# Expert sizes for every set, unscaled token rows, centred weights in DRAM and a folded skip term in a two-layer mixture-of-experts kernel

## The chip, the cores and the metric

The kernel runs on one core of a Trainium2 chip. The metric is the time of one execution on the device in microseconds. A core has a matrix engine (TensorE, in the profile PE, with its weight loads as PEld), a vector engine (VectorE, DVE), a scalar engine (ScalarE, ACT), a general engine (GpSimd, POOL) and a queue engine (SyncE, SP) that issues transfers here. Each takes its own instructions strictly in order; what one engine makes for another is announced with semaphores.

## The reference

The input x is 16 sequences of 256 tokens with 128 features, 4096 tokens in all. Four steps follow one another, with residual additions.

```python
# 1 attention: the softmax over m sums to one and v does not depend on m
att = softmax(q k^T * scale, axis=2)
opt = einsum('blmh,blhd->blhd', att, v)          # = v
x = x + opt_of(layernorm(x)) @ w_out.T + b_out

# 2 and 4: a mixture of experts, the same weights both times
n = layernorm(x)
logits = n @ gate_w                              # 8 experts
top2, weights = top-2 of logits, softmax over the two
x = x + sum_i weights_i * relu(n @ w1[e_i]) @ w2[e_i]   # 128 -> 512 -> 128

# 3 a selective-scan mixer (W_x, W_dt, A_log, D, W_out, b_out)
y = scan(u, delta, A, B, C) + u * D              # the skip term
x = x + y @ W_out.T + b_out
```

The above is cut to what matters: attention reduces to a linear map of the normalised tokens; each token goes to the two of eight experts with the highest logits, and what the experts return is weighted by a softmax over the two; the mixer's last term is the input u scaled by D for each feature.

## The kernel before

**Blocks and sets.** The 4096 tokens are 8 blocks of 512 (four tiles of 128 tokens each). A mixture-of-experts layer does not run over all blocks at once. It runs over sets of blocks: in layer 1 the sets are [0], [1], [2,3], [4,5], [6,7] (`FIRST`, L28), in layer 2 [0,1], [2,3], [4,5], [6], [7] (`SECOND`, L29). `layer` (L1679) does for each set: what comes before (attention, or the gate of layer 2), `route`, `experts`, and then what comes behind: `arrive` (L1659, return of the experts' rows and the mixer) in layer 1, `finish` (L1667, return, transposes and output) in layer 2.

**Routing.** `choose` (L1156) finds the two highest logits of each token as one-hot rows and the softmax factors p. A few bf16 multiplications count, for every token, how many tokens ahead of it in the set chose the same expert. From this comes a slot for each of the token's two experts. `route` (L1330) then makes a normalised and scaled row of the token for each of the two, (x − mean) · rstd · p, on ACT or DVE (tile `row`), and an indirect transfer on POOL (`scatter`, L876, seen as L880) writes 128 such rows at a time to their slots in a DRAM buffer `slots`. As relu passes a positive factor, scaling a row by p is the same as weighting what the expert returns.

**Experts.** Every expert has a fixed number of slots in a set, given by `SLOTS` (L32) as rows and columns, (108, 3) being 324 slots; the program's matrix shapes follow from it, and not from the counts of the run. `experts` (L1389) fetches an expert's slots to the tile `xs` (SP), transposes them (into `ps_b`, copied to `xsT`), multiplies by the four 128-wide parts of w1 (the up multiplications, into `ps_B` or `ps_b`), applies relu on ACT or DVE (`h`), multiplies by the four parts of w2 (the down multiplications, into `ps_y`), transposes back (`yT`, `ps_b`, `yr`) and stores the rows to a DRAM buffer `ys` (SP). For some sizes the down multiplication is turned round and gives rows at once (`ps_y<-w_s,h`). The weights of all eight experts stay in on-chip memory (`w1_s`, `w2_s`). Set [0] of layer 1 is dealt with otherwise: `dealt` (L1316) makes a one-hot matrix of slots and tokens for each expert (`u<-ramp`) and multiplies, with no transfer.

**Return.** `collect` (L1446) fetches, for each block and each of the two choices (a half), four times 128 rows of `ys` by indirect transfers on POOL (`gather`, L889, seen as L892) into the tile `yy`, and adds the 128x512 tile to x on DVE or POOL.

**Ranked sizes.** In layer 2 the sizes in a set differ from expert to expert. `ranking` (L1253) sorts the experts by their counts in the first set of layer 2 and the order holds for all its sets (`RANKED`, L44). `load_experts` (L921) therefore loads the weights a second time in that order, 16 transfers of 256 KB, whose source address is read from a register (a `value_load` on SP for each expert). In layer 1 all experts have the same size in a set.

**Order.** All work is first recorded as jobs of a `Plan` (L239) and then emitted in an order that is packed in the string `ORDER` (L62): a rank for each job. The plan's own durations (`cost`, and those given with `scatter`, `gather`, `move`) decide which engine takes a job that several could do, and how long TensorE is expected to idle ahead of a job. Where that is over 0.5 us, multiplications of zeros are sent in their place, one for 0.26 us (L1705, here called fillers); within the first 5 us (`COLD`) half as many. A memset of one element (L1711) stands between neighbouring indirect transfers of one kind. As all instructions are issued by one helper, nearly all lines of the profile are L772, and tiles tell the groups apart.

**Fallback.** If a count exceeds its slots, or a bound that the mixer's shortened scans rest on fails, a second program (`general`, L433) computes everything again (L1718 to L1730).

Of the kernel before, what the change touches and what calls it, by code (L numbers as in the profile page):

```python
# [11 lines left out]
BF16 = mybir.dt.bfloat16  # L12
# [7 lines left out]
P = 128  # L20
# [12 lines left out]
    {  # L33
        "first": ((88, 2),) * 8,
        1: ((84, 2),) * 8,
        2: ((108, 3),) * 8,
    },
    {
        "first": ((126, 3), (112, 3), (108, 3), (98, 3), (96, 3), (88, 3), (126, 2), (117, 2)),
        1: ((98, 2), (91, 2), (88, 2), (80, 2), (84, 2), (75, 2), (70, 2), (128, 1)),  # L40
        2: ((126, 3), (117, 3), (110, 3), (104, 3), (108, 3), (96, 3), (90, 3), (126, 2)),
    },
)
RANKED = (2,)  # L44
UNIT = 2
JOIN = 2

COLD = 5.0
# [14 lines left out]
    "c-qZZ2V4_p|G(!F2uWCBZ^GVNMD}nMWhmmpRjsY4t)oufI_lQiswi$nt>RvFf>K)%!~%*UB1=HoJFEa1cmE`Jxw{}(`+wi}^LZ0U"  # L63
    "a?kVJZ+?H@-|v>G_^I*=>c6NNCEAl^pxer^W>rkfI9&R;>iv%8rd7`B9lu02joA1NUDGqgsne+5m*>sC|3s_)i)v%K>WE364%f`z"
    "G%9VWd>|BeK0IC08FfuyS$#TV!ssUsJvZ9pw@tBaV2TlOKM(^Ype&9CWvPXsXYyKG+Pu%zXlZI1Sm&A}IY4CALbDer*&iR4gwV&l"
    "%_}jzc_s5zX!X3PvIWf#4x)X!&c}M*s#~aW*_FM4<>R>>-Ss7LRsE&oXUE3!i@n2)%YK;$2Ux%Q=KJd&AzO97EXmqll<=(G$|n86"
    "dYcDRExkEyN=&Uj^@^>Aca=O|2u`0WZ*KkZPp*nx>bjin<VsZC<o=9uRhFUFl+z=MPhNm~zw4pXzFM^_s$-IHUykn8ElEaxc^26-"
    "@4I$-U9_@v4^`W~w0Z1KeP?YmwJLUVr{|Jk*2t*vvi=>escnr%S2%5T@YvyUd1cK_&1T~j6D^|8^}R6ZVc4@5r`2UVu#9lkK^d>j"
    "<5raWMYj1fEzYZOy26KDMUnzv7Ki#3$Js3MGeWdkH_RQX!$+g^SGwX*L0g)m*&ht^hr`B{m+-Z+MtiQ=%kQlyO?ID9`_|x>g>x4a"
    "7{0aWT9KvwE7Mny<Gx<_BC^rwXq|G-%~+*L?XOC-N_X*TlWs>d*t>6dr4MgmZ>V5Cdl#UwvuaJIa7A;6SkO9NyAy2)R#I*_c4irG"  # L70
    "f$}i1aA)c7s#VilXwygk=1!Yh4K5@zA4WBp!hdS2*QXZDe|&PBD<YV-*P?Y!iDl#0qE3S>ix*QK?M<<E=x(XAp(VMh1?XG@R;LUe"
    "^+r5mvX*|O{~BSeh+)#r_1}t5_Zhr&a6Vyi`WybF4oh}yO!N4+5htCOsU-6w+usb|b1Ki@BBPCK;{T?1ty+gYBRIVexWd-=;yaSJ"
    "&s)c$pQk1Mu(kK>{gXydj2^f9i*!A>vkJ$Aory7?vCXs9d*QbqY<=vPD_5viZHRw+xyi_Maei$clW%G}<<Bhkhz`r&MH-;Cg^e&a"
    "U3gYoEtvixd0S^(bWqX_ezZ?DQW4gCxKZW)U-sXiwFV<^9XWugj&I$OH!^<jINSI_Rp(0X8CAy1J2}<+XY8MsQOzx+FI`ck!)UF1"
    "r{3=xWR>+`>d7lshLx35&odZn7Zx}mrDnxJanplDErz>)?7F~R3+C+aA5-pJSJA{omZhmanOZhgkCAfdi0_(u)pB)q^G@34(G14f"
    "eS4#Xe51_BB9U#NK~YP9t>|iZM^tyo*>WS%F&D1MxJN(sPW#RtZCBBJZJ^)!epUT0n_AeiD}P#^{fyO-2NJ+a(?751T|Dt?cbC&s"
    "Vc(n$QTC>HM#at;b;t51I;SD3MmT%!f%h}4>PBvxuFe>3;@b3@A8^VmYfe%~m6J|SeG|jhc2S6Tkp)nnb$DNx$-9k@&62&})9eDh"
    "ScjD#Mm+6S`}*KmrOj)ty&MV-D)rOH_rKCv)^PRbMmOGYj!yTV8??Q`+N`UlY#O%f5B};74O>|C*7x@ozso+too$4EyDPAtJ-2Le"
    "uTEEI%<mI*o7jdlVWH_fj=;E{yK8^RlKf4p9e+HX@qI@>qK&dre+c0=@TMCTa6xyst-wJ;H>2N&$y}<c%!q`U@CUzomIp^G>DPJt"
    "S!x=E$jI-zmAMAtYp?dBF3J<a_^i}!9^FgHm{tEc#Gh9&w{A|0ef5VbPi>8y1=e34J|A%@QR|nJJQv~V+30jzx^DxA@33*RbCs>%"  # L80
    "ef3A`HOopwyjkjeHH}(F$Ieng4b!X;HExa5f1%a}jGt%hF>5F+ZFknJV%x@_61{ioY8P?EddV{*+HUb(fS#Qbt)^2r^(WJ`)UPYu"
    ")JFWl;98WeIb=8Tk2<=R1-&Pa79=`8w;g#um40nvvTte-sCm{D_|vkM$>|}6bRG!cYgMZ0^S*OreBm=TH+%Z~Jcp5~?Y_@P(9st@"
    "2CsX<E{?mh@~%t6aDJ(4L*w;>xy$qNjg9mfd=Ae^*L+-(bAJ8d=)3ycVdKZQ%egm9ODFqhX5N_LFyCI_K3f0nvJ^FDW!RAzPKVo+"
    "&IIVELnF5YsV!Rmvh`YcsoiL^-lwHm!S_vG?p9glT3%@%v(D~K^6D*%ik-FG(>9-*)PGiwXO`l5rF63Hy$X+bo)u_IOW1QRTiI}<"
    "<_VqfqH_^joC>Np-yO~piB@y!^DI<vt(p<a79|+4%EN6Q+BDz2GK+27_hV+{U*BnPFSKTUHNV=Vhjk($xUov;CwT7HHq%es;o@7v"
    "s~x8lM&||AjNuQ<wZ6Bmwd>bY8~1<UXj(W%Ur`$cXWJOv-;lnhYT8?FUx$uYp|x^`un9G&o1Iu;t!dRW&g^Bb=_0hyX(rG0_x5<J"
    "W}lxb*X~)HAE-1pB;BQ^LG!O|{!7wateXuPjy1g47G;AAOE#v|-`IO4l;JX=Le)SmG4aUQQQ6kXA%1z9t<NK0dmq^jAGBJpuKxgd"
    "eXkawFZ5$JMr2mlKB{8c=h)_Zy$KD=PPGs%xvk#g-~MD_9aH;}d%czM@ozmdc5X7%n7k(1V&fu#xkh5jB_tPq;C45@tIXzkaGgr;"
    "`U-V}elJ1K5|2t9!%F4Ie79N)zMgFdqAF5lr;az799pBdl=r?p=s{9t<;`CXoASO{t7VrlBRG@0J_1I0K8Wt`_lI$swmu6BI^+PG"
    "R<t`R#ilQeDPFoWaTfD_W-45&V`fle={DiT+;e$tuyA_JGv2os@98-1FqqaFKEJbL>3+MFs}kA@zjoxM2@bBZ-Zv|~*-qnO412%B"  # L90
    "Hrl?39I;U2Nl)*kc{(>WG8$)ax|gm~8_)17zHBvazRBVuOO~Pjb<fxgT5}Y$rBU13yY<|T>gT@6y{t2fvzNc1KieD~H?c3yIG5%1"
    "EZC;L<sGZu9pMPV16%ccCfxd9<XECrYvkB!<h1ocr=`%<`N@intL=VX)*h7_ooi=p!&4c>U}btmTfv<omWIQ-a$8N>Cfiq*;mz*K"
    "X~Rn9R^2?n+niWz_x`eL{ozpO&1-+YWLh^$VDQqHpSVriI0n@^F|pk#E1}=9&or)NWV*op*e;vXrU5-JJxh-3Fk{-vL_ZWd-(`H2"
    "k@>2&TjXi*rq>P$e>>}7fV!t%UxR&U@8s&d;UV$g>F5|2Zpc2S=4zO^Jm5y+3zK*Htk~qyL5(?+wC+!_Zq6Cy`MkJ=^V`TyeWuXt"
    "&YapiOGBTs*#<0g<ztSzO#Mb4*Oi?TS!SZ4o^E#ZOhD4zQ=R+|Ixbw%HSS}*_Wf~Z>nrHuK4p{B+fH~UE>nKqtaR_P_PR4V=)GIP"
    "!Ikr-C#gjoJ>T&4m`N)*+szxBUi?zstQE)^-*auA<Lrx}7Gn-|ZG9f9D$<H~iw)(J4uc)c&AfL9uaDPpx~_b%G&X4U1Ad5jy|0kt"
    "-q%m7eTec@?E3E4PPX$n(aU-rFg1Mb6W;3N3jQ<IiG33%{1O-0xc2P#Mc2LUH4C!)1d=i2$+S8jbn2MmrUfI44!n=6D`;&|bw8)y"
    "MfYYF)pRR$)vNK;YU^v8rn%{zpSh*DMQ>#O<%u3}gHdkWyZcHxnY}jZ*J4i7EpLtfqkWEhOIbWuuiJ~hV{K6Q^&if?00DY0hVOmz"
    "w(r2s*FMAf{wuvbzY9&%5hrHsZXcB!Frs-!vd?v~)$Q@#yhiOE3(d+F)HQFI-@S##Q8iU@>%DG>IK7Hv8*S0w$rzhkaXC6o)ji8s"
    "`!Bs^j7RVnPN~uUeqGnob@xW?s`toU?B})Hci%{(+x}N#%V$Pprx$y2*!ij>)2t(qr7We8OpgM4w#&%LI@|8^R%NLE{xFwj+K}6m"  # L100
    "b#UGJVz!Frr07J=%-<$(E^!5ZPiC$>cICE-+9D&MvC_q=&c?IIp#PomyfstNq`8xn_PPi{-i^Qb^B4icKWSfnWuEpshKGMXO-KBa"
    "=BoRm!22z7$df~xYih~RD4J0_uHf#=@y4}b4=0M=y}F&4Z()!27mYJDP#W|4r2qBc5k6+ZsmEp;lr-B_g}@On;%JxdtZy7=+QdGx"
    "yla*QO+TGe7qCPrt6tNs!1LsF+YX1c?FNBPU%_hnsIm6g1-Z(n%9a$4aLcXI(=D#wS?k^4&KOZ*`&&}y{2h1Nf(s*Ou)a7J-V;=5"
    "`P4q4-{LJlR5<M0=6>%|UzTqL+sN`e7sJ_KZg8@&@au7ONDB*z{gWFQUT1pQv}Vx+x9Hik#V7Rl+Z)hgxUIJA$4R$lKR?^2v3_#!"
    ">)PnR%R2jnzwLTu3Uu|kbtp<>T=OyQvM-&@w&$T@l}_3ZQ*NSLbH51^?E9;{t@f*o)tW*1N!vbj^|Lw3#=Yep4jt^mESpJxfC&!u"
    "_j<e<oHm85F<l%mC!pg^x#5;03HD#!nfc|W!Yv&~&3er&Hy#Y)c(sHwV#d^Ud=anS!QbqV|0JrT#@hFbW6e=28?RYgY;T}n^*esh"
    "+f#V-iGLybGSv_*tJ;;?#RTx?(>iSLS`GI|w-ybT=8a5-_S(Yg$bBX;2j0eVis|qA3g-E?KhJwV&Eu78T5)&z_y-)N`nxw$=*&I4"
    "nhaG+6Gw5t#PeFdh8BM?nN!+Kv}|TAVpYGdJksWFbWPdEPrax`*`nI_smPJjoW9V~)4$rh{Hwd?rzM>5KH{xeU~?{qv)X@bwaNGe"
# [553 lines left out]
def tile_layers(  # L662
# [43 lines left out]
    def room(k, blocks):  # L706

        first = blocks == routed[k - 1][0]
        return SLOTS[k - 1]["first" if first else len(blocks)]
# [1066 lines left out]
```

## Time and profile before

| | us |
|---|---|
| runs | 472.38, 471.61, 468.14 |
| median | 471.61 |
| profiled execution | 467.84 |
| its span, first to last instruction | 466.1 |
| TensorE clock granted, mean | 0.994 |
| last up multiplication of the sets of layer 1 | 62.4, 87.3, 129.8, 181.4, 242.0 |
| last up multiplication of the sets of layer 2 | 311.8, 355.7, 399.9, 422.3, 442.8 |
| first one-hot tile of set [0] | 21.3 |
| first up multiplication | 27.7 |
| reloads of the weights for layer 2 issued | 206.1 to 246.5 |
| moved by DMA | 55.37 MB |

Times of events are those of the profiled execution, counted from the start of the span. A group of the profile has its line, engine, operation and tiles, then output and input shape, the number of instructions, and behind the bar the busy time in us and the mean of one in ns; behind the second bar stands how long the engine idled just before such instructions, and what ended that.

### The profile page before, as it was taken

What the parts mean: (1) busy time and instruction counts of PE and PEld (TensorE: products, weight loads), DVE (VectorE), ACT (ScalarE), POOL (GpSimd) and SP (SyncE); (2) the same over time, 40 slices, a digit from 0 to 9 for tenths busy, and PEclk for the clock granted to TensorE, in tenths of its full rate; (3) what the DMA queues carried; (4) which work ended last, traced back from release to release, by engine and by line L of the source; (5) the groups of instructions that cost most, each with busy time, mean ns of one, the idle gap of its engine ahead of it and who ended that gap; (6) DMA issues with size and microseconds to landing.
All of it is one profiled execution on the core that took longest, in us unless ns stands there. A gap on an engine that the chain in (4) does not pass through costs nothing.

```text
span 466.1 us, 8797 instructions
## 1 busy us (share of the span) xinstructions
PE 447.0 (96%) x2670; PEld 355.8 (76%) x2670; DVE 345.6 (74%) x1229; ACT 268.3 (58%) x621; POOL 311.8 (67%) x482
## 2 busy tenths in 40 slices
PE   8999999999999999989997999989999999999994
PEld 6889998866766667665665777677678877999993
DVE  4799999778697878999999998996786931223420
ACT  2124443577576854995889496797735534343310
POOL 8188787777673761276866776836785477778662
PEclk9999999999999999999999899999999999999999
DMA  5974234632352423236644322144225333543251
GB/s 155 340 244 135 71 122 134 166 107 66 108 155 67 114 78 96 65 106 195 188 121 142 93 73 76 53 120 132 69 58 146 114 113 90 135 125 91 78 164 45
DMA packets 74917, 55.37 MB, mean 119 GB/s; under 512 B 8184, under 2 KB 66800, under 8 KB 74864
## 3 DMA queue, kind: packets, MB, share of 16 engines
q1 hardware_dynamic: 66640, 38.35, 28.5%
q0 software_dynamic: 7936, 16.27, 12.1%
q8 instruction: 23, 0.38, 0.4%
q14 instruction: 30, 0.25, 0.2%
q10 hardware_dynamic: 288, 0.13, 0.1%
HBM read 28.95 MB, written 25.77 MB: 117 GB/s over the span
## 4 chain that ended last, share of the span: by engine, by line
PE 72%; DVE 16%; ACT 4%; issue 3%; POOL 2%; DMA 1%; POOLq 0%; DVEq 0%; ACTq 0%
PE ps_b L772 25%; PE ps_y L772 24%; PE ps_B L772 21%; DVE x L772 3%; DVE ps_B L772 2%; DVE stats L772 2%; PE ps_y L1705 2%; POOL yy L892 2%; DVE w L772 1%; DMA yy<-ys,of 1%; DVE th L772 1%; ACT th L772 1%; DVE rt L772 1%; ACT decay L772 1%; DVE u L772 1%
## 5 line engine op out<-in xcount | busy, mean ns | idle before, releaser
L892 POOL DMA_INDIRECT yy<-ys,of x128 | 125.5, 980 | 64.4 <-issue 37.2
L880 POOL DMA_INDIRECT slots<-row,to x120 | 120.6, 1005 | 49.5 <-issue 19.4
L772 PE MATMUL ps_y<-h,w_s 128*128 128x324 f32 (+13 forms) x552 | 145.2, 382 | 0.0
L772 PE MATMUL ps_B<-xsT,w_s 128*128 128x324 f32 (+9 forms) x352 | 112.8, 442 | 0.8 <-DVE w L772 0.4
L772 PEld LDWEIGHTS ps_y<-h,w_s 128*128 128x128 f32 x552 | 90.4, 190 | 20.3 <-issue 1.3
L772 PEld LDWEIGHTS ps_B<-xsT,w_s 128*128 128x128 f32 x352 | 61.7, 191 | 23.8 <-issue 3.2
L772 ACT ACTIVATE h<-ps_B 128x648 f32<-128x648 f32 (+9 forms) x62 | 43.8, 707 | 33.5 <-PE ps_B L772 33.1
L772 PE MATMUL ps_b<-xsT,w_s 128*128 128x176 f32 (+9 forms) x288 | 54.8, 316 | 1.2 <-ACT yr L772 1.2
L772 PEld LDWEIGHTS ps_b<-xsT,w_s 128*128 128x128 f32 x288 | 44.1, 190 | 2.7 <-ACT yr L772 1.5
L772 ACT COPY yT<-ps_y 128x324 f32<-128x324 f32 (+14 forms) x52 | 18.8, 362 | 36.0 <-PE ps_y L772 35.2
L772 ACT ACTIVATE th<-later,lneps,ha_s 128x112 f32<-128x112 f32 (+13 forms) x85 | 39.1, 507 | 0.2 <-DVE th L772 0.2
L772 ACT ACTIVATE h<-ps_b 128x352 f32<-128x352 f32 (+9 forms) x47 | 22.3, 474 | 26.0 <-PE ps_b L772 24.1
L772 PE MATMUL ps_b<-ident,yT 128*108 128x128 f32 (+11 forms) x177 | 34.4, 274 | 0.7 <-ACT yr L772 0.7
L772 ACT COPY xsT<-ps_b 128x324 f32<-128x324 f32 (+15 forms) x52 | 19.1, 372 | 26.6 <-PE ps_b L772 25.3
L772 ACT ACTIVATE decay<-delta,nea 128x108 f32<-128x108 f32 (+13 forms) x85 | 31.7, 412 | 2.7 <-DVE delta L772 2.6
L1705 PE MATMUL ps_y<-blank,ones_d 128*128 128x128 f32 x232 | 31.2, 293 | 1.3 <-DVE blank L772 1.3
L772 DVE TENSOR_TENSOR_SCAN w<-decay,ps_B 128x360 f32<-128x360 f32 (+7 forms) x40 | 31.0, 802 | 1.3 <-ACT decay L772 0.5
L1705 PEld LDWEIGHTS ps_y<-blank,ones_d 128*128 128x128 f32 x232 | 30.0, 208 | 1.6 <-DVE blank L772 1.3
L772 ACT COPY yr<-ps_b 108x384 f32<-108x384 f32 (+13 forms) x50 | 21.3, 425 | 16.8 <-PE ps_b L772 16.8
L772 ACT ACTIVATE row<-x,mp,rp 128x128 f32<-128x128 f32 x63 | 28.1, 488 | 3.6 <-DVE rp L772 2.0
L772 PE MATMUL ps_b<-ident,xs 108*128 108x108 f32 (+13 forms) x186 | 29.7, 256 | 0.1
L772 DVE TENSOR_SCALAR h<-ps_B 128x648 f32<-128x648 f32 (+6 forms) x26 | 21.3, 819 | 11.1 <-PE ps_B L772 10.8
(207 smaller groups left out, 792.2 us busy)
## 6 DMA issues: line engine op xcount, KB each, us to landing
w_s<-in_w SPq DMA_DIRECT2D x32, 256.0 KB
xs<-slots SPq DMA_DIRECT2D x27, 162.0 KB
ys<-yr SPq DMA_DIRECT2D x27, 162.0 KB
slots<-blank SPq DMA_DIRECT2D x2, 1280.0 KB
xT<-in_xT SPq DMA_DIRECT2D x8, 256.0 KB
yy<-ys,of POOLq DMA_INDIRECT x128
out_T<-xnT SPq DMA_DIRECT2D x8, 256.0 KB
slots<-row,to POOLq DMA_INDIRECT x120
```

The lines of the kernel that those rows point to most:

```text
L772: return lambda: f(*[real(x) for x in a], **{n: real(x) for n, x in k.items()})
L880: inst = nc.gpsimd.indirect_dma_start(out=real(out), out_offset=bass.IndirectOffsetOnAxis(ap=real(rows), axis=0), in_=real(in_), in_offset ...
L892: nc.gpsimd.indirect_dma_start(out=real(out), out_offset=None, in_=real(in_), in_offset=bass.IndirectOffsetOnAxis(ap=real(rows), axis=0),)
L1705: nc.tensor.matmul(out=spare, lhsT=ones_d.real(), rhs=blank.real(), start=True, stop=True,)
```

## The change

- **Sizes.** `SLOTS` has an entry for every set. In layer 1 the sets [2,3], [4,5] and [6,7] have sizes by rank (2201, 2328 and 2328 slots in place of 2592 each); layer 2 has 2348, 2464, 2464, 1263 and 1263 in place of 2370, 2505, 2505, 1300 and 1300.
- **Rankings.** The experts are ranked at set [2,3] of layer 1, for this and the following sets of layer 1, and at the first set of layer 2. Each ranking is followed by a reload of all weights. All eight register values are read in one step.
- **w1 centred.** At the first load each w1 is multiplied by the centring matrix on TensorE and copied back; the token rows then keep their mean. Centred w1, and w2 in the layout of on-chip memory, are stored to DRAM (`w1c`, `w2c`), and the reloads read these in runs of 2 KB.
- **Rows.** `scatter` writes the tokens' rows of x as they are. The factor p · rstd (`share`) is applied on return: four operations of 128x128 for each half, x + yy · share, in place of one addition.
- **Layout.** An expert's slots are one contiguous piece of `slots` and `ys`. A token beyond its expert's slots goes to a row of its own behind them (two more operations of a routing).
- **Set [0].** rstd of block 0 comes from a power on POOL; the one-hot tiles hold ones and may be made by ACT too (two activations).
- **Skip term.** u is scaled by 2 · D, the scan's part is added to it, and one multiplication by W_out/2 takes the place of two.
- **Plan.** Some durations change, the halving of early fillers goes, and `ORDER` is new.

The counts of the two programs' main instructions, without the fallback: matrix multiplications 1968 and 1978 (fillers 116 and 134 among them); DVE 1185 and 1252; ACT 706 and 654; POOL 490 and 542. Scatters are 120 and gathers 128 in both.

```diff
@@ tables
+    (   # layer 1
+        ((88, 2),) * 8,
+        ((84, 2),) * 8,
+        ((108, 3), (99, 3), (94, 3), (90, 3), (89, 3), (87, 3), (128, 2), (122, 2)),
+        ((106, 3), (103, 3), (98, 3), (97, 3), (95, 3), (94, 3), (94, 3), (89, 3)),
...
-RANKED = (2,)
+RANKED = ((1, 2), (2, 0))
-COLD = 5.0
@@ def load_experts
+                pw = bank("B", P, FF)
+                matmul(pw, centre, into[0])
+                copy(into[0], pw)
+                move(w1c[r], into[0], 4 * P * FF, took=0.5, turn="centred")
+                move(
+                    w2c[r], into[1].rearrange("p c d -> p (c d)"), 4 * P * FF, took=0.5,
+                    turn="centred",
+                )
...
-                said.append(nc.sync.value_load(which.real()[0:1, r : r + 1], min_val=0, max_val=NE - 1))
+                seen = plan.job([("SP", 1.0, look)], [], [which], turn="weights")
...
-                    in_=w2[bass.ds(said[0], 1)].rearrange("o (c p) d -> p (o c) d", p=P),
+                    in_=w2c.real()[bass.ds(said[r], 1)].rearrange("o p (c d) -> p (o c) d", d=P),
@@ def dealt
-            k = (hot[:, t], ramp.rearrange("p c k -> p (c k)"), at[:, t, e : e + 1], m[:, 0, t, e : e + 1],
-                 ALU.is_equal, ALU.mult)
-            either(("DVE", "tensor_scalar", k, {}), ("POOL", "tensor_scalar", k, {}))
+            k = (hot[:, t], count, at[:, t, e : e + 1], None, ALU.is_equal)
+            either(
+                ("DVE", "tensor_scalar", k, {}), ("POOL", "tensor_scalar", k, {}),
+                ("ACT", Away, (hot[:, t], count, at[:, t, e : e + 1], one_c), {}),
+            )
@@ def route
+            past = small("rest", n, NE)
+            V.tensor_tensor(past, at[:, 0:n], spread(lies[:, 1], n), ALU.is_ge)
+            V.scalar_tensor_tensor(at[:, 0:n], past, BIG, at[:, 0:n], ALU.mult, ALU.add)
...
-                r = new("row", [P, NTT, P], bufs=ROW)
-                for t in range(NTT):
-                    w, m = (v[:, i, lo + t : lo + t + 1] for v in (rp, mp))
-                    either(
-                        ("ACT", "activation", (r[:, t, :], xs_[b][:, t, :], AF.Identity),
-                         dict(bias=m, scale=w)),
-                        ("DVE", "tensor_scalar", (r[:, t, :], xs_[b][:, t, :], w, m, ALU.mult,
-                                                  ALU.add), {}),
...
-                        q.slots, idx[:, i, lo + t : lo + t + 1], r[:, t, :], f"in{q.name}",
+                        q.slots, idx[:, i, lo + t : lo + t + 1], xs_[b][:, t, :], f"in{q.name}",
@@ def collect
-            product(xs_[b], xs_[b], y, ALU.add)
+            for t in range(NTT):
+                V.scalar_tensor_tensor(
+                    xs_[b][:, t, :], y[:, t, :], q.share[:, i, lo + t : lo + t + 1],
+                    xs_[b][:, t, :], ALU.mult, ALU.add,
+                )
@@ def mixer
-            matmul(so, wsd_s, u[:, i], True, False, hold=[sos])
-            matmul(
-                so.rearrange("p (s l) -> p s l", l=L)[:, :, L - KM : L], wsh_s,
-                whole[:, NSEQ * i : NSEQ * i + NSEQ], False, True,
-            )
+            either(
+                ("ACT", "activation", (u[:, i], u[:, i], AF.Identity), dict(scale=skip2)),
+                ("DVE", "tensor_scalar", (u[:, i], u[:, i], skip2, None, ALU.mult), {}),
+            )
+            own = slice(NSEQ * i, NSEQ * i + NSEQ)
+            product(ends[:, own], ends[:, own], whole[:, own], ALU.add)
+            matmul(so, wsh_s, u[:, i], hold=[sos])
```

## The prediction

> **What bounds the kernel now.** I read the first rows of the page, then the chain that ended last, then the busy time in stretches cut at the ends of the expert sets, and last the groups of TensorE and VectorE. First the page: engines, then two rows of tenths in 40 slices, then the chain by engine.
>
> ```profile
> PE 447.0 (96%) x2670; PEld 355.8 (76%) x2670; DVE 345.6 (74%) x1229; ACT 268.3 (58%) x621; POOL 311.8 (67%) x482
> ...
> PE   8999999999999999989997999989999999999994
> ...
> DVE  4799999778697878999999998996786931223420
> ...
> PE 72%; DVE 16%; ACT 4%; issue 3%; POOL 2%; DMA 1%; POOLq 0%; DVEq 0%; ACTq 0%
> ```
>
> TensorE is full nearly everywhere and holds 72% of the chain. VectorE is second, full from about 180 to 290 us and slack at the end. The stretches show where TensorE is not really at work (columns: stretch, then busy us of PE, PEld, DVE, ACT, POOL; clock; DMA share; GB/s):
>
> ```profile
> 0.00:28.00 28.00, 24.10 (x136) 21.29 (x137) 18.64 (x105) 5.01 (x16) 16.55 (x103) 1.00 0.89 261
> 28.00:62.00 34.00, 33.34 (x237) 31.69 (x237) 33.05 (x204) 15.39 (x42) 26.46 (x37) 1.00 0.41 123
> 62.00:87.00 25.00, 24.56 (x188) 23.39 (x187) 23.80 (x139) 12.30 (x36) 18.93 (x30) 1.00 0.49 136
> ...
> 181.00:242.00 61.00, 58.49 (x297) 39.47 (x297) 58.38 (x167) 50.32 (x105) 35.03 (x45) 1.00 0.44 126
> 242.00:262.00 20.00, 17.43 (x105) 13.61 (x104) 19.32 (x38) 16.10 (x32) 14.71 (x14) 0.93 0.51 148
> ...
> 443.00:466.10 23.10, 16.19 (x143) 15.68 (x140) 3.79 (x6) 2.35 (x6) 10.85 (x12) 0.96 0.34 105
> ```
>
> Some of that busy time is filler (L1705, multiplications of zeros sent where the plan expects TensorE to idle): 9.45 us of it before 28 us, 8.06 between 181 and 262, 12.83 after 443, hardly any elsewhere. So there are three places where something else sets the pace: the start (loads, DMA share 0.89, and the routing of the first block), 181 to 262 us (VectorE busy 77.7 of 81 us under the mixers), and the tail (eight gathers 1.25 us apart on POOL, a landing of 2.59 us, then an addition, transposes and the output). Everywhere else a column less on TensorE is time won. Prices of TensorE, by shape:
>
> ```profile
> L772 PE MATMUL ps_B<-xsT,w_s 128*128 128x324 f32 x216 | 69.3, 442 | 0.6 <-DVE w L772 0.4 <-DVE var L772 0.3
> L772 PE MATMUL ps_b<-u,wsd_s 128*128 128x512 f32 x16 | 8.3, 600 | 0.0
> L772 PE MATMUL ps_b<-th,wsh_s 128*128 128x360 f32 x16 | 6.3, 474 | 0.0
> L1705 PE MATMUL ps_y<-blank,ones_d 128*128 128x128 f32 x232 | 31.2, 293 | 1.3 <-DVE blank L772 1.3
> ```
>
> 27 fetches of 324 rows with 4 up multiplications each are 108 instructions but 216 records, so every fp32 multiplication makes two passes. From 324 to 512 columns a record grows by 158 ns over 188 columns: 0.84 ns a column and pass, 1.68 ns a column of a multiplication, 0.84 of a one-pass transpose.
>
> **The change, part by part.**
>
> *Fewer slots.* Rows over all experts and sets fall from 20508 to 19411, by 1097: 391 in set [2,3] of layer 1, 264 in each of [4,5] and [6,7], 178 in layer 2. Up multiplications lose 4 × 1097 = 4388 columns, 7.4 us; down ones 4284 (some work by rows and keep their width), 7.2; transposes 1097 in and 1024 out at 0.84 ns, 1.8. Together −16.4 us of TensorE.
>
> *Skip term folded.* Per block a 512-column and a 360-column multiplication become one of 512: 8 × 360 × 1.68 ns = −4.9 us. In return there are eight scalings of u (seven on ACT, one on DVE) and eight additions of whole (five DVE, three POOL), priced below.
>
> *w1 centred once.* Eight 512-column multiplications, 0.86 us each: +6.9 us. Five stand ahead of the first expert, in the stretch with 9.45 us of filler, so I charge nothing for those 4.3; if that cover goes (the weights landing too late for them), they cost it. The other three stand among the first experts: +2.6 on the path. Their eight copies go to ACT (7) and DVE (1); ACT is busy 20.4 of the first 62 us.
>
> *Fillers.* 116 become 134. A 128-column filler takes 2 × 0.11 = 0.22 us: 18 are 4.0 us. They stand where the new order expects idle time, so they cost between nothing and 4.0; I charge all 4.0, as a sign that the new order itself expects that much more waiting.
>
> *Rows unscaled, factors on return.* All 120 row operations go, and two operations in each of the ten routings that made their factors. Each of the 32 halves that come back now needs four 128x128 operations on DVE in place of one 128x512 addition, which stood 20 times on DVE and 12 on POOL:
>
> ```profile
> L772 DVE TENSOR_SCALAR row<-x,rp,mp 128x128 f32<-128x128 f32 x57 | 18.3, 353 | 0.1
> ...
> L772 DVE TENSOR_TENSOR x<-x,yy 128x512 f32<-128x512 f32 x20 | 14.1, 705 | 17.4 <-DMA yy<-ys,of 17.4
> ...
> L772 DVE SCALAR_TENSOR_TENSOR x<-ps_B,rstd,x 128x128 f32<-128x128 f32 x32 | 10.4, 344 | 3.5 <-PE ps_B L772 3.5
> ```
>
> The nearest row is the last (same operation and shape): 128 × 0.344 = 44.0, less 14.1 and 18.3, is +11.6 us of DVE. Copies change engine too: eight fewer h of two banks (−6.6), ten more xsT (+4.2), ten more yr (+5.0), eight more th products (+2.8), five fewer one-hot tiles of set [0] (−2.0). DVE's sum is +15.0, 361 us in all; ACT loses 28.1 of rows and some 6 of copies. Over the span that is hidden: DVE has 120 us of slack. It isn't between 181 and 262, where five halves return: 20 × 0.344 = 6.9, less three additions at 794 ns there (2.4), less five row operations (1.8), is +2.7 us, which I charge in full. The ends are −1.8 (only the rows count, POOL and ACT take the rest) and +5.5 (twice my price).
>
> [...]
>
> *Second ranking, 2 KB runs, spill rows.* The ranking moves to the third set of layer 1 as well, with 16 more reloads of 256 KB from a DRAM copy that 16 new stores write first: 8.4 MB on top of 55.37. Two small DVE operations are added per routing (about 0.2 us each by the 128x64 rows), nine times, and some ten of the second ranking: hidden where DVE waits. SP's queue carries all of it in order: three pairs of stores stand ahead of, and others between, set [0]'s ys stores and set [1]'s xs fetches, and so does the look at the order of experts, which waits for the ranking. Before, the counting of [2,3] came at 52 us and [1]'s fetches at 56, so the look should be answered in time. A weight buffer is free after its expert in [1] (3.1 us each, from 64) and wanted in [2,3] (5 us each, from 90): 23 us of slack for the first, growing. I take 0; the ends are 0 and the whole 4.2 MB waiting (below).
>
> *Tail.* The last operation after the last gather is 128x128 (344 ns) in place of 128x512 (690): −0.4, with −0.1 for the first copy: −0.5.
>
> **Sum.** −16.4 − 4.9 + 2.6 + 4.0 + 2.7 − 0.5 = −12.5 us on the span of 466.1, so 453.6; with the 1.7 us around it (profiled execution 467.84) 455.3. The median of the runs shown stands 1.0081 above that execution: **459 us**.
>
> **Rivals.**
>
> *DVE takes what TensorE gives.* From 181 to 242 DVE has 2.6 us of idle time, so shorter experts of [6,7] (264 rows × 15 ns = 3.9 us) and five of eight folded skip terms (3.1) may only make TensorE wait. That loses 7.0, and DVE's extra at the upper end another 2.7: −2.8 on the span, (463.3 + 1.7) × 1.0081 = **469**. For it: those 77.7 of 81 us. Against: most of [4,5] and all of layer 2 after 312 us lie outside.
>
> *The weights' round trip (slower).* If reloads cannot run beside set [1] and come only at its end, 4.2 MB at the 261 GB/s of the first stretch take 16.1 us, a landing 2.6, less the 2.7 between 87.3 and the next set's first up multiplication at 90: 16 us of TensorE waiting ahead of [2,3], and up to 24 if the stores (another 4.2 MB) are half still queued. (453.6 + 16 to 24 + 1.7) × 1.0081 = 475 to 483, middle **479**. It decides once a reload lands more than 23 us after its buffer is free. For it: DMA was already at 0.41 and 0.49 in the two stretches concerned, and stores, looks, fetches and reloads share SP's queue. Against: 261 − 136 = 125 GB/s are free, and the reloads have from 66 to 125 us, which asks for 71.
>
> *The start comes earlier.* If the one-hot tiles (POOL 0.99 us each, 20 of them, after 10.1 us idle for DVE's shares) no longer hold set [0] back, the fillers cost nothing and some 4 us of the start goes: 453.6 − 4 − 4 + 1.7, × 1.0081, is **451**.
>
> That the change doesn't do what it says could only mean the fallback: a set whose counts pass the tighter slots is computed a second time by another program. The input is fixed and its counts by the reference's rule stay under every size given, so this gets no chance.
>
> **How the numbers follow.** Forecast (454 to 465) 0.50; DVE bound 0.17; round trip 0.20; earlier start 0.13. A measurement can tell about 1% here, 466.9 to 476.3. Faster: 0.48 of the first, 0.05 of the second, the last: 0.66. Same: 0.02, 0.12 and 0.03: 0.17. Slower: the rest of the round trip, 0.17. The range of 8 in 10 goes from 448 (under the earlier start) to 474 (above DVE bound with one of its terms larger); what it leaves out is nearly all of the round trip.
>
> **What would show it.** TensorE's records of 324 columns give way to those of each expert, and its busy time without fillers falls by 14 us; the last up multiplication of [2,3] comes 3 to 6 us before 129.8 and that of layer 2's last set 12 before 442.8. DVE is at 360 us, ACT near 240. A round trip shows as TensorE idle ahead of the first up multiplications of [2,3], released by a DMA of w1c or w2c. I am wrong most likely if the stretch from 181 to 262 grows, or if the first 90 us do.

## The result, and the profile after

| | before | after |
|---|---|---|
| median of four runs each, us | 470.31 | 552.86 |
| ratio to before, 95% interval | | 1.175 (1.166 to 1.184) |
| profiled execution, us | 467.84 | 551.57 |
| its span, us | 466.1 | 549.6 |
| TensorE clock granted, mean | 0.994 | 0.933 |
| transfers `xs<-slots` and `ys<-yr`: median from issue to last landing, us | 2.9 | 7.2 |
| the longest of them, us | 4.8 | 22.2 |
| the longest issue of one on SP, us | 1.2 | 6.9 |

The kernel became 17.5% slower, where I had forecast 2.7% faster (459 against 471.61 us). Some later comparisons fell in jobs in which the kernel before itself took 633 to 645 us; they stand at the end of the experiments. The first rows of the page of the kernel after are these.

```profile
span 549.6 us, 8897 instructions
...
PE 455.8 (83%) x2702; PEld 365.3 (66%) x2702; DVE 354.2 (64%) x1293; ACT 251.1 (46%) x572; POOL 285.6 (52%) x534
...
PE   8999999799807998659883699995998979987785
...
DMA  8974689413112211121933112212233223332241
```

No engine has become the bound: TensorE falls from 96% to 83%, VectorE from 74% to 64%. TensorE has fewer columns to multiply, yet its busy time without fillers is not shorter: 455.8 less 39.2 is 416.6 us, at a mean clock of 0.933, against 415.8 us before, at 0.994. The span has grown by waiting. The first 87 us go nearly as before, though the stores of the weights raise the DMA share from 0.41 and 0.49 (columns as in the prediction: stretch, busy us of PE, PEld, DVE, ACT, POOL, clock, DMA share, GB/s):

```profile
28.00:62.00 34.00, 33.82 (x242) 31.48 (x242) 32.91 (x214) 17.48 (x49) 23.22 (x42) 1.00 0.60 194
62.00:87.00 25.00, 24.82 (x187) 23.76 (x186) 20.43 (x111) 8.62 (x26) 17.59 (x22) 1.00 0.78 244
```

After that there is a hole in nearly every set, and the loss adds up over the whole rest of the run: the last up multiplication comes 3 us later than before in layer 1's [2,3] (133.2 against 129.8), 35 in [6,7] (276.6 against 242.0), 59 in layer 2's [2,3] (414.9 against 355.7) and 81 in the last set (523.9 against 442.8). The largest hole lies between 150 and 170 us:

```profile
140.00:150.00 10.00, 9.66 (x45) 6.24 (x43) 3.72 (x14) 4.60 (x9) 0.00 (x0) 1.00 0.19 65
150.00:160.00 10.00, 0.99 (x5) 0.53 (x5) 0.00 (x0) 2.97 (x5) 0.00 (x0) 0.73 0.11 41
160.00:170.00 10.00, 1.64 (x5) 1.29 (x6) 2.43 (x7) 0.00 (x0) 5.78 (x6) 0.50 0.19 56
170.00:180.00 10.00, 10.00 (x45) 7.22 (x44) 6.70 (x18) 5.83 (x12) 7.77 (x8) 0.91 0.18 50
```

All engines stand still for most of it, and the DMA engines are nearly idle too: 0.11 of sixteen engines is less than two. The granted clock falls within the hole, after TensorE has stopped, and is back at full between 170 and 180 us (0.56 from 170 to 172, 1.00 from 172 on); what TensorE waits for, below, is data and not the clock. The chain of waits of this run is of no help, since it breaks off after a few per cent, so I took the waits by engine (us in total, times, the longest):

```profile
DVE x L787 <- DMA yy<-ys,of: 80.0, 26, 20.0
POOL yy L922 <- DMA ys<-yr: 78.6, 6, 29.4
PE ps_b L787 <- DMA xs<-slots: 30.4, 10, 7.3
```

Before, POOL waited for the stores as follows, VectorE 17.4 us for gathered rows (the row of `x<-x,yy` in the prediction), and TensorE for fetches not at all:

```profile
POOL yy L892 <- DMA ys<-yr: 17.7, 3, 14.2
```

The timeline of the hole shows the links (start, us, engine, line, operation; in brackets the idle time before and what ended it):

```profile
149.29 2.50 SPq L787 DMA_DIRECT2D ys<-yr  x1
151.89 3.80 SPq L787 DMA_DIRECT2D xs<-slots  x1
153.01 0.47 PE L787 MATMUL ps_b<-ident,xs 95*128 95x95 f32 x3 [3.36 <-DMA xs<-slots]
...
162.49 0.97 POOL L922 DMA_INDIRECT yy<-ys,of  x1 [29.35 <-DMA ys<-yr]
...
167.52 0.35 DVE L787 SCALAR_TENSOR_TENSOR x<-yy,share,x 128x128 f32<-128x128 f32 x1 [19.98 <-DMA yy<-ys,of]
...
168.36 0.67 PE L787 MATMUL ps_b<-ident,yT 128*106 128x128 f32 x2 [14.35 <-DVE w L787]
```

The fetch that TensorE transposes at 153.01 was issued at 142.99: 10 us for 142 KB. The store issued at 149.29 lands at 161.70, the gather behind it starts at 162.49, VectorE gets its rows at 167.52, then comes to what the mixer needs, and TensorE goes on at 168.36. The queue engine itself is held up: one issue takes 3.80 us. The tile view of the fetches says the same for all 72 (least, median and most ns of an issue), of the kernel before and of the kernel after:

```profile
L772 SPq DMA_DIRECT2D xs<-slots x72: 350/800/881, 56.1 to 426.2; - x72
```

```profile
L787 SPq DMA_DIRECT2D xs<-slots x72: 216/362/6903, 50.8 to 506.8; - x72
```

The median issue became cheaper and the worst eight times dearer. So I sorted the transfers by their number of rows (the partitions of the tile), and counted in the trace how often each of them moves its semaphore, the counter by which its landing is announced. A weight load of 128 rows moves it 16 times. A fetch of 103 rows issued at 125.10 moves it twice: at 125.70, and at 138.24 when it has landed. Over all 152 fetches and stores of the kernel after:

```
rows                             updates of the semaphore    largest divisor up to 16
80, 96, 128                              16                        16
90                                       16                        15
84, 98, 126                              15                        14
117                                      14                        13
72, 108                                  13                        12
88, 99                                   12                        11
95, 115                                   6                         5
124                                       5                         4
87, 123                                   4                         3
86, 94, 106, 122                          3                         2
83, 89, 97, 103, 107, 109, 127            2                         1
```

(A few transfers show an update less; fewer of 84 rows show 14.) The count is the largest divisor of the rows up to 16, and one more where that is below 16. I read that divisor as the number of engines among which a transfer is dealt out in equal shares. No view names a transfer's engines, but the landings in the hole fit. After 153.34 us, the last update of a store of 128 rows, four transfers under way make theirs one after another: two fetches of 94 rows at 156.22 and 159.10, the store of 122 rows at 161.70, the fetch of 89 rows at 167.30. Each comes 2.9, 2.9, 2.6 and 5.6 us after the one before it, and half the bytes of the first three transfers, and all of the fourth's, make 24 or 25 GB/s over these times. From 155 to 162 us the DMA share is 0.11, 1.8 of sixteen engines.

By that reading the kernel before had all 152 transfers on 11 to 16 engines; its trace shows 11 or more updates for 142 of them and fewer for ten, of shapes that show 13 or more elsewhere in the same trace, which I take for missing records. The kernel after has 72 there (median landing 4.2 us), 50 on two to six (9.8 us) and 30 on one (10.5 us). These are numbers of one execution with the queues as they were; the experiments have to show that the count is the cause.

### The profile page after: what moved, and what is told of

Read it like the earlier page. It is cut to its first block, busy times and chain, and to the rows that moved or that the text cites. A ratio compares the mean times of both kernels' runs of the same rounds, so it can differ in the third digit from the quotient of the medians.

```text
span 549.6 us, 8897 instructions
## 1 busy us (share of the span) xinstructions
PE 455.8 (83%) x2702; PEld 365.3 (66%) x2702; DVE 354.2 (64%) x1293; ACT 251.1 (46%) x572; POOL 285.6 (52%) x534
## 3 DMA queue, kind: packets, MB, share of 16 engines
q0 software_dynamic: 7936, 16.27, 10.5%
## 5 line engine op out<-in xcount | busy, mean ns | idle before, releaser
L922 POOL DMA_INDIRECT yy<-ys,of x128 | 123.0, 961 | 169.4 <-DMA ys<-yr 78.6
L910 POOL DMA_INDIRECT slots<-x,to x120 | 117.2, 976 | 43.0 <-issue 25.9
L787 PE MATMUL ps_y<-h,w_s 128*128 128x176 f32 (+21 forms) x528 | 137.0, 373 | 0.5 <-DVE h L787 0.5
L787 PE MATMUL ps_B<-xsT,w_s 128*128 128x282 f32 (+17 forms) x336 | 111.8, 452 | 9.8 <-DVE th L787 8.7
L787 DVE SCALAR_TENSOR_TENSOR x<-yy,share,x 128x128 f32<-128x128 f32 x128 | 42.9, 345 | 80.5 <-DMA yy<-ys,of 80.0
L787 ACT ACTIVATE h<-ps_B 128x564 f32<-128x564 f32 (+14 forms) x66 | 44.5, 677 | 95.2 <-PE ps_B L787 79.0
L787 PE MATMUL ps_b<-ident,xs 94*128 94x94 f32 (+25 forms) x182 | 32.7, 263 | 35.3 <-DMA xs<-slots 30.4
L787 PE MATMUL ps_b<-xsT,w_s 128*128 128x176 f32 (+12 forms) x304 | 59.3, 321 | 2.3 <-DVE h L787 1.2
L787 PE MATMUL ps_b<-ident,yT 128*88 128x128 f32 (+19 forms) x169 | 36.8, 285 | 17.6 <-DVE w L787 14.4
L1779 PE MATMUL ps_y<-blank,ones_d 128*128 128x128 f32 x268 | 39.2, 297 | 3.3 <-ACT yT L787 1.6
L1779 PEld LDWEIGHTS ps_y<-blank,ones_d 128*128 128x128 f32 x268 | 36.8, 212 | 6.9 <-ACT yT L787 2.6
L787 ACT ACTIVATE th<-later,lneps,ha_s 128x112 f32<-128x112 f32 (+14 forms) x85 | 39.6, 508 | 0.0
L787 PE MATMUL ps_y<-w_s,h 128*122 128x128 f32 (+6 forms) x232 | 33.5, 283 | 2.1 <-DVE h L787 2.1
```

The lines of the kernel that those rows point to most:

```text
L787: return lambda: f(*[real(x) for x in a], **{n: real(x) for n, x in k.items()})
L910: inst = nc.gpsimd.indirect_dma_start(out=real(out), out_offset=bass.IndirectOffsetOnAxis(ap=real(rows), axis=0), in_=real(in_), in_offset ...
L922: nc.gpsimd.indirect_dma_start(out=real(out), out_offset=None, in_=real(in_), in_offset=bass.IndirectOffsetOnAxis(ap=real(rows), axis=0),)
L1779: nc.tensor.matmul(out=spare, lhsT=ones_d.real(), rhs=blank.real(), start=True, stop=True,)
```

## The experiments

Theory A: the row counts decide on how many engines a fetch or a store goes, and everything lost comes from that. Theory B: VectorE, with four operations for each returning half. Theory C: the weights' round trip through DRAM. Theory D: the new order of the work does not fit the times that the work takes on the chip.

What ran beside a kernel before of 633 to 645 us is at the end of this part. All else stands beside one of 470 us.

**Splitting the transfers.** The sizes, the matrix work, the order and the plan stay; a transfer whose rows are no multiple of 16 goes out in two pieces.

```diff
+    def move_parts(out, in_, size, took, **order):
+        n = out.shape[0]
+        m = n // 16 * 16
+        whole = [out] if m in (0, n) else [(out[0:m], in_[0:m]), (out[m:n], in_[m:n])]
...
+            for o, i in whole:
+                nc.sync.dma_start(out=real(o), in_=real(i))
...
-                move(x, q.part(q.slots, r), 4 * N * P, took=0.55, turn="fetch")
+                move_parts(x, q.part(q.slots, r), 4 * N * P, took=0.55, turn="fetch")
...
-            move(q.part(q.ys, r), yr, 4 * N * P, took=0.55, key=f"out{q.name}")
+            move_parts(q.part(q.ys, r), yr, 4 * N * P, took=0.55, key=f"out{q.name}")
```

> The changed kernel with its own sizes; every fetch of slots and every store of expert rows whose row count is not a multiple of 16 goes out as two transfers, the first with the largest multiple of 16, the second with the rest. Nothing else moves, and the plan does not know of it. Theory A: 455 to 475 us; some 120 issues more on the queue engine, 0.3 us each, which it has time for. Theories B, C and D: 553 us, or more by the issues.

Measured: 461.15 us, 0.980 (0.977 to 0.984) of the kernel before. The page:

```profile
span 459.3 us, 9103 instructions
...
PE 436.8 (95%) x2702; PEld 353.9 (77%) x2702; DVE 353.8 (77%) x1293; ACT 249.8 (54%) x572; POOL 287.6 (63%) x534
```

TensorE has the same 2702 instructions as in the kernel after, and the holes are gone; transfers land in 2.0 us (median, 6.4 at most). Nothing of B, C or D was touched, and all of the loss and more came back: 91.7 us of the median. This is shown, then: the changed kernel loses by how these transfers are cut, and the runs below, which leave the transfers whole and change only their rows, tie it to the row count. Split, it is 2% faster than the kernel before.

**Splitting the fetches alone.** The same with only the first of the two replaced lines.

> As the kernel with both split, but only the fetches of slots are split, the stores of expert rows are as in the changed kernel. Theory A: about half of the gain, 490 to 530 us, with the gathers still waiting for stores and TensorE no longer for fetches. Theories B, C, D: 553 us.

Measured: 488.54 us, 1.040 (1.037 to 1.044). The fetches bring back 64.3 of the 91.7 us, more than the half I expected and just outside my 490 to 530 us; the stores, split after them, bring the other 27.4. TensorE waits for fetches directly (30.4 us in the kernel after); for the stores it is the gathers at the end of a set that wait (78.6 us on POOL).

**Odd rows in the kernel before.** 109 in place of 108 rows, three columns each, for the experts of layer 1's sets of two blocks.

```diff
-        2: ((108, 3),) * 8,
+        2: ((109, 3),) * 8,
```

> The kernel before with 109 instead of 108 rows (times 3) for every expert of the sets of two blocks in layer 1: 72 slots more, 1.1 us of TensorE. Theory A: 109 is prime, so 24 fetches and 24 stores of 327 runs of 512 bytes go through one engine, some 9 us each in place of 3, and the sets of layer 1 wait for them: over 490 us. Theories B, C, D: 471 to 473 us.

Measured: 733.52 us, 1.558 (1.552 to 1.564). 24 fetches and 24 stores now move their semaphore twice and no more. From issue to landing these fetches take 21.0 us (median) and these stores 18.5, where I had expected some 9, and the queue engine spends 405 us in the issues of the 152 transfers in place of 121. The waits and the tile view of the fetches:

```profile
PE ps_b L772 <- DMA xs<-slots: 118.4, 15, 22.2
```

```profile
L772 SPq DMA_DIRECT2D xs<-slots x72: 347/837/9936, 57.6 to 693.2; - x72
```

One row more in 24 of 80 expert passes, 1.1 us of work, costs 263 us. It needs neither the new layout of `slots` nor anything else of the change. The plan had moved some instructions for the new size, so the same was also run in exactly the order of the kernel before (below, beside a slower kernel before).

**Raising the sizes.** 39 of the 64 sizes by rank go up by one to four rows, to one with a divisor from 11 to 16 (115 excepted): 168 slots of 19411. The expectation's 24 counts equal sets once and is one too many.

```diff
-        ((106, 3), (103, 3), (98, 3), (97, 3), (95, 3), (94, 3), (94, 3), (89, 3)),
+        ((108, 3), (104, 3), (98, 3), (98, 3), (96, 3), (96, 3), (96, 3), (90, 3)),
...
-        ((124, 3), (117, 3), (108, 3), (103, 3), (106, 3), (94, 3), (88, 3), (122, 2)),
+        ((126, 3), (117, 3), (108, 3), (104, 3), (108, 3), (96, 3), (88, 3), (126, 2)),
```

> The changed kernel with 24 of its expert sizes raised by one to four rows of tokens, each to the next one with a divisor between 11 and 16 (103 to 104, 106 to 108, 97 to 98, 94 to 96, 89 to 90, 122 to 126 and so on; 115 is left): 168 slots more of 19411, 2.5 us of TensorE by 15 ns a slot. Theory A (a transfer of n rows is spread over the largest divisor of n up to 16 engines, so that 103 rows go through one and 94 through two): 455 to 470 us, fetches and stores landing in 2 to 4 us, TensorE's waits for fetched rows gone. Theory B (VectorE, with four operations a half on return) and theory C (the weights' round trip through DRAM): nothing of theirs is touched, so 553 to 558 us. Theory D (the new order of work does not fit the chip): the order changes a little, 540 to 560 us.

Measured: 524.47 us, 1.118 (1.113 to 1.122), neither theory's number. The transfers are mended here: no issue over 1.8 us, fetches in 1.8 to 6.2. But TensorE has far more fillers (the group of L1779, first in this run and then in the kernel after):

```profile
L1779 PE MATMUL ps_y<-blank,ones_d 128*128 128x128 f32 x694 | 87.3, 281 | 2.6 <-ACT yT L787 1.3
```

```profile
L1779 PE MATMUL ps_y<-blank,ones_d 128*128 128x128 f32 x268 | 39.2, 297 | 3.3 <-ACT yT L787 1.6 <-DVE blank L787 1.3 <-ACT yr L787 0.5
```

347 fillers in place of 134: the plan itself expected TensorE to idle that much. The ranks in `ORDER` do not fix the order; the plan replays the work with its own durations and the ranks choose among what is ready. With other sizes other jobs are ready at other moments, and the same ranks gave a poor order. So theory D may hold for this kernel, by my edit and not by the change. The next run takes it away.

**Raising the sizes in the changed kernel's order.** The order, the choice of engines, the buffers and the fillers of the changed kernel are written into the kernel as a table, so that only the sizes differ from it.

```diff
-        end, start, way, buffer = self.made = self.forward(*self.ranks())
-        for h, b in zip(self.homes, buffer):
-            if b is not None:
+        d = zlib.decompress(base64.b85decode(FROZEN))
+        order = [int.from_bytes(d[2 * i : 2 * i + 2], "little") for i in range(n)]
+        way = [("PE", "DVE", "ACT", "POOL", "SP")[x] for x in d[2 * n : 3 * n]]
+        fill = d[3 * n : 4 * n]
```

> The raised sizes in the changed kernel's order, a third time, since the kernel before itself took 633 and 644 us in the two jobs so far. Theory A: 457 to 466 us beside 470 for the kernel before. If the sizes themselves cost the 524 us: about 520.

Measured: 460.34 us, 0.980 (0.977 to 0.983) of the kernel before. The span is 457.6 us, the fillers are 37.3 us of TensorE, and the engines:

```profile
PE 437.5 (96%) x2702; PEld 353.0 (77%) x2702; DVE 353.9 (77%) x1293; ACT 250.6 (55%) x572; POOL 287.4 (63%) x534
```

Sizes with good divisors mend the kernel without a split, for 168 slots, and 64 us of the run before were its order, with the choice of engines and the fillers that came with it.

**The operations on return, twice.** On the kernel with both splits, each of the 128 operations is done a second time into a scratch tile.

```diff
+                nc.vector.scalar_tensor_tensor(scratch, *(real(x) for x in v), ALU.mult, ALU.add)
                 once()
```

> Each of the 128 operations on return done twice, with the split transfers, whose own kernel gave 461.2 us: 466 to 470 us by my price (hidden except from 181 to 262 us), 475 or more if VectorE binds from 130 to 312 us, 461 to 463 if it is hidden everywhere. The earlier runs of it fell on disturbed chips.

Measured: 485.93 us, 1.035 (1.029 to 1.041), 24.8 us above the kernel with both splits and in the range that I had named for a VectorE that binds from 130 to 312 us. Where they went can be read from the same stretch of work in both, from the last up multiplication of layer 1's [2,3] to that of layer 2's [2,3]: 127.5 to 348.0 us in the split kernel and 130.7 to 371.8 in this one.

```profile
127.50:348.00 220.50, 211.06 (x1209) 157.24 (x1209) 203.28 (x584) 150.75 (x328) 136.66 (x184) 1.00 0.34 100
```

```profile
130.70:371.80 241.10, 218.87 (x1209) 160.90 (x1209) 224.65 (x649) 151.04 (x326) 134.75 (x181) 0.98 0.30 91
```

The same 1209 instructions on TensorE; VectorE is busy 21.4 us more and the stretch is 20.6 us longer. VectorE is at 92 and 93% there. So what was added to VectorE over the middle, and not only from 181 to 262 us, lengthened the span nearly one for one. Whether that is its load, or only that these operations stand in the way of the next set's work, this run does not tell apart, nor what less work on VectorE would gain. In the kernel before VectorE was busy 198.0 us, 88%, from 130 to 356 us.

Theory B had named the right engine, but it is no part of the 82 us lost: with the transfers split the four operations are all still there.

**Beside a slower kernel before.** In three jobs the kernel before took 633, 644 and 645 us; why is not known, and it does not go with the chip, since the one of the second job had given 470 us earlier. The raised sizes in the changed kernel's order and the doubled operations were run again later beside 470 us (above). Three edits ran nowhere else. One is the 109 rows in the order of the kernel before. One has 108 rows again for layer 1's experts with three columns, with the raised sizes elsewhere and in the same order:

```diff
-        ((108, 3), (104, 3), (98, 3), (98, 3), (96, 3), (96, 3), (96, 3), (90, 3)),
+        ((108, 3),) * 8,
```

The third reads the reloads of w2 in runs of 512 bytes, on the kernel with both splits:

```diff
-                    in_=w2c.real()[bass.ds(said[r], 1)].rearrange("o p (c d) -> p (o c) d", d=P),
+                    in_=w2[bass.ds(said[r], 1)].rearrange("o (c p) d -> p (o c) d", p=P),
```

The first job, beside 633 us:

> The kernel with the raised sizes once more, but every engine's instructions in exactly the order of the changed kernel, with its choice of engines and its 134 fillers (the raised sizes alone had let the plan come to another order, with 347 fillers). Theory A, with the 524 us of the raised sizes put down to their order: 457 to 466 us, as with the split transfers, 2.5 us more of TensorE and fewer issues. If the 524 us came from the sizes themselves, or transfers matter less than the split suggests: about 520 us.

> As the raised sizes in the changed kernel's order, but every expert with three columns in the sets [2,3], [4,5] and [6,7] of layer 1 has 108 rows again as before the change (12 engines a transfer): 699 slots more. TensorE as the bound everywhere: 699 x 15 ns = 10.5 us more than the raised sizes in that order. VectorE as the bound from 181 to 262 us: the 234 slots of [6,7] are hidden there, 7 us more. No value in the smaller sizes: the same time.

> The kernel with both kinds of transfers split, and each of the 128 operations on return done twice, the first time into a scratch tile: 44 us of VectorE more, with the result unchanged. My price (hidden except from 181 to 262 us, where five halves return, 6.9 us): 466 to 470 us. VectorE as the bound over the whole middle from 130 to 312 us: 475 us or more. VectorE hidden everywhere: 461 to 463 us.

> The kernel with both kinds of transfers split, with the 16 reloads of w2 read from the input in runs of 512 bytes, as before the change, and not from the copy in runs of 2 KB (the copy is still stored). The round trip and its run length hidden: 459 to 463 us. Reloads on the path: 470 us or more.

Measured, as ratios to the kernel before: raised sizes 1.041 (1.029 to 1.052), 108 rows again 1.041 (1.019 to 1.063), operations twice 1.054 (1.042 to 1.066), runs of 512 bytes 1.033 (1.022 to 1.044). The second job, beside 644 us, with 109 rows in the order of the kernel before:

> The raised sizes in the changed kernel's order, again, as the chip of the runs before gave the kernel before itself 633 us, a third above its usual time. Theory A: 457 to 466 us beside a kernel before of 470. If the sizes themselves cost the 524 us: about 520.

> 108 rows for the three-column experts of layer 1 again, in the changed kernel's order, again: 10.5 us more than the raised sizes if TensorE is the bound everywhere, 7 if VectorE hides [6,7], nothing if smaller sizes are worth nothing.

> Each of the 128 operations on return done twice, with the split transfers, again: 466 to 470 us by my price, 475 or more if VectorE binds from 130 to 312 us, 461 to 463 if it is hidden everywhere.

> The kernel before with 109 for 108 rows in layer 1, as in the earlier run, but with every engine's instructions in exactly the order of the kernel before. Theory A: near the earlier 733 us, above 650, since the engine count and not the order made it slow. If its order did: 471 to 480 us.

Measured: raised sizes 1.028 (1.009 to 1.047), 108 rows again 1.039 (1.015 to 1.063), operations twice 1.042 (1.022 to 1.061), 109 rows 1.319 (1.292 to 1.346), 843 us. The third, beside 645 us:

> 108 rows for the three-column experts of layer 1, in the changed kernel's order, a third time: 10.5 us above the 460.3 us of the raised sizes if TensorE is the bound everywhere, 7 if VectorE hides [6,7], nothing if smaller sizes are worth nothing.

> Each of the 128 operations on return done twice, with the split transfers (461.2 us), a third time: 466 to 470 us by my price, 475 or more if VectorE binds from 130 to 312 us, 461 to 463 if it is hidden everywhere.

> Reloads of w2 in runs of 512 bytes from the input, with the split transfers (461.2 us), again: 459 to 463 us if the round trip and its run length are hidden, 470 or more if reloads are on the path.

> 109 for 108 rows in layer 1 of the kernel before, in its own order, again: above 650 us by theory A, near the 733 of the first run; 471 to 480 us if the order had made that one slow.

Measured: 108 rows again 1.023 (1.015 to 1.031), operations twice 1.033 (1.026 to 1.040), runs of 512 bytes 1.020 (1.013 to 1.027), 109 rows 1.318 (1.309 to 1.328), 847 us.

The times in microseconds that I had expected were meant beside 470 us and can't be held against these. The raised sizes are 3 to 4% above the kernel before here and 2% below it beside 470 us, so these ratios don't carry over, and what the smaller sizes and the run length of the reloads are worth by themselves stays open. Only the 109 rows stand far outside of all intervals, in an order that is exactly that of the kernel before: as far as these jobs can show it, the order is not what slowed them in the run above.

## Why the prediction was wrong, point by point

**The step that failed** is the one under "Fewer slots". I counted a row as 15 ns of TensorE and left the fetches and stores of those rows as the trace of before had them: some 3 us each, for sizes of 108, 126, 98 or 84 rows; what the new row counts do to them stands in my sum as nothing, without a reason. In that trace the time of a transfer depends little on its size (medians of the fetches from 2.2 to 3.8 us), and every size there has a divisor from 11 to 16. The change picks sizes by counts alone: 97, 103, 89, 107, 127. The term that is missing is +92 us on the span (549.6 against 457.6 with raised sizes in the same order), against all the gains together of 12.5. The kernel before held the hint: all of its 152 transfers have row counts with a divisor from 11 to 16, and its trace has the updates from which the use of it is seen.

**My slower rival had the wrong mechanism.** It expected a wait for reloads at set [2,3], at a DMA share near the 0.89 of the start. From 100 to 260 us the share is 0.11 to 0.36: the DMA engines were not short of bandwidth, most of them had nothing to do. The 32 reloads of 128 rows move their semaphore 16 times each (15 in three records), so by the same reading they used all sixteen engines, and with the transfers split the whole round trip was still there while the loss was not. The mark I named for it, TensorE idle ahead of [2,3] behind a DMA of w1c or w2c, did not appear: TensorE's first wait for a transfer there was for `xs<-slots`, 3.7 us at 104.

**The sum itself was nearly right once the transfers are mended.** I had −12.5 us on the span (the folded skip term is 4.8 us by its own factors and not 4.9), and with 2.5 more for the 168 slots −10.0. Raised sizes in the same order give 457.6 − 466.1 = −8.5; split transfers −6.8, with 140 issues more. Term by term:

- TensorE: 437.5 busy less 37.3 of fillers is 400.2, against 447.0 less 31.2, 415.8, before: −15.6, where I had −14.4 and with 168 slots −11.9. The ends of matmuls are modelled in the profile, so this is as near as the views allow. In the kernel after itself the fall by 14 that I had named as a sign does not show: it is 416.6 against 415.8.
- Fillers: 6.1 us busy more (31.2 to 37.3); I had charged 4.0, at 0.22 us for one, where my own row (31.2 us for 116) has 0.27.
- The start: the first expert's first up multiplication at 28.8 us in place of 27.7; I had it at no change, and the earlier start that I gave a chance did not come. The last up multiplication of set [0] comes 4.2 us later than before (66.6 against 62.4), that of [1] 1.6 later (88.9 against 87.3), where I had charged 2.6 for the centring.
- VectorE: 353.9 us in all where I had 361 (its +15.0 was +8.3), and ScalarE 250.6 where I had near 240. The operation on return takes what I had priced it at, 345 ns against 344; the group in the kernel after:

```profile
L787 DVE SCALAR_TENSOR_TENSOR x<-yy,share,x 128x128 f32<-128x128 f32 x128 | 42.9, 345 | 80.5 <-DMA yy<-ys,of 80.0
```

Its price on the path was probably mis-sized: I charged 2.7 us because I let it bind only from 181 to 262 us, though my own rows have it 33.05 of 34 us busy from 28 to 62 and at eights and nines in all slices from 186 to 315. The doubled operations cost nearly one for one from about 130 to 350. What the whole change adds there I cannot separate; at one us for one, the 5 us by which the same stretch of it is busier than before (198.0 from 130 to 356, 203.3 in the split kernel) is of the size of what is missing: the other terms as measured, −15.6 and the 4.3 of centring that I had as covered, +6.1, +1.1 and −0.5 for the tail as I had it, give −13.2, and the span gave −8.5. That is an argument from a few numbers and not shown by a run of its own.

- The last up multiplication of layer 1's [2,3] came 3.6 us before that of before (126.2 against 129.8), inside the 3 to 6 that I had named; that of the last set 7.8 before (435.0 against 442.8) and not 12. Where the difference arises is not shown.
- The look at the order and the stores in SP's queue, priced at nothing: with raised sizes the 72 fetches take 323 ns each to issue (median) and none over 723, so nothing held the issues up.

**The range and the chances** failed with the step: I had given slower 0.17, all of it to a mechanism that did not act. That the rest of the sum came out within 2 us is in part luck: TensorE's busy time fell by 3.7 us more than I had forecast, and fillers, start and probably VectorE took it back.

## What to carry to other kernels

Before a size of a tile is made smaller, look at what else is cut by it. Here the largest divisor up to 16 of a transfer's rows tells, as I read the updates, on how many DMA engines it runs: sixteen for 96 rows (16 updates), one for 97 (2), and a saving of 15 ns a slot on TensorE was paid for with some 7 us a transfer (medians of 9.8 us on two to six engines and 10.5 on one, 2.9 before). Count the updates of the semaphore for one transfer of each shape, round the size up or send the remainder separately; and when an order of work was searched for certain sizes, freeze it before testing others, or the test measures the order.

## What the runs showed of the hardware that I had not expected

- Several transfers on one or two engines held up the queue that issues them. In the kernel with 109 rows a single issue took up to 9.9 us, in the kernel after up to 6.9, and before 1.2 at most. In the kernel after 18 issues took over 2.5 us, each with at least two transfers of one or two engines ahead of it that had not landed; with the fetches split and the stores left whole, none took over 2.0. Transfers of good sizes come late with them: the 72 on 11 to 16 engines landed in 4.2 us in the kernel after, and the same 72 in 2.3 with raised sizes.
- Transfers whose rows are one contiguous run each were much cheaper to issue: with raised sizes the 152 fetches and stores took 50.9 us of the queue engine, 0.34 each, in runs of 1 to 1.5 KB for most, where the kernel before took 121.2, 0.80 each, in runs of 512 bytes. Within the kernel before, the four with one run a row took 0.35 to 0.53 us, those with two or three 0.59 to 1.21. They also landed sooner, 2.3 us against 2.9. What of this is the layout and what the number of runs is not separated.
- The granted clock fell after TensorE had been idle: 0.73 and 0.50 in the two stretches of the largest hole and 0.91 in the next, 0.933 over the kernel after, 0.83 with 109 rows, and 0.998 again with the transfers split or the sizes raised in the same order.
